# Coefficient tiles in DRAM laid out by row pairs instead of by single steps

## The chip, the cores and the metric

The kernel runs on one core of one Trainium2 chip. The metric is the device time of one execution in microseconds. Before the change it is 2900.72 us, the median of three runs (2892.87, 2900.72 and 2903.77). The profiled execution took 2902.61 us.

## The reference

Four layers run over x of shape (4, 64, 256, 256) in float32: batch, channels and images of 256 x 256. Layers 0, 2 and 3 are long convolutions with separable filters; layer 1 works on Haar coefficients. Cut to what matters:

```python
# layers 0, 2, 3: hx, hy are (256 x 64) filters from a small sine network
k = einsum('ijk,imk->ijmk', hx, hy)[0]            # separable per channel
y = irfft2(rfft2(x, 512, 512) * rfft2(k, 512, 512))[..., :256, :256]
out = y + x * bias[:, None, None]                  # causal 2-D convolution
# layer 1
f1 = haar2d(x)                                     # all levels, rows and columns
for i in range(2):
    f4 = einsum('bchw,oc->bohw', f1 * v[i], conv_w[i])      # mixes the 64 channels
    acc += sign(f4) * relu(abs(f4) - tau[i])
y = haar2d(acc, inverse=True) + x
```

The convolutions and the Haar transforms work on one image of one channel. The mixing of layer 1 needs all 64 channels of a coefficient row at once.

## The kernel before

The batch is cut into GROUPS = 2 groups of NB = 2 images. Each group has ROUNDS = 32 rounds of CI = 2 channels, so that a round holds four images: 128 partitions of 2048 floats (8 KB). The first 64 partitions belong to the round's first channel and the others to its second (`half(e)`).

Three phases follow one another, and overlap:

- **Phase A** (64 rounds): for each round, load x (L133), convolve rows and columns as Toeplitz products on TensorE (L307), add the bias term (L470), run the Haar transform along the free dimension on GpSimd (L355, L357) and along the partitions on TensorE (L319), copy the result to a tile f (L483), and store f to the DRAM tile coef of its group (L488, in `store`).
- **Phase B** (64 steps per group): a step has all 64 channels of two coefficient rows: 128 partitions (row, channel) of NB x 512 floats, 4 KB. `load` brings ft from coef (L546) and v and tau (L552). Two units per step mix the channels on TensorE (L592), multiply by v (L603), and apply the threshold (L609 to L619). GpSimd adds the two branches and the old coefficients (L629, L632), and the sum gt is stored to the DRAM tile mixed (L635).
- **Phase C** (64 rounds): load g from mixed (L699), run the inverse Haar transform (L375, L392, L394, L319), and then the two convolutions of layers 2 and 3 (L307), and store the output (L766).

So coef is written in rounds (two channels, all rows) and read in steps (two rows, all channels); mixed is written in steps and read in rounds. Each of the four DRAM tiles (coef and mixed of two groups) holds 64 x 512 KB, 32 MB.

Every DMA is issued from SP's queue, in the order in which the kernel's Python code runs; there is no scheduler behind it. Phase A of group 1 runs beside phase B of group 0, and phase B of group 1 beside phase C of group 0; `beside` interleaves the pieces of two lists by count. In a round the SP queue gets six loads of Toeplitz filters (tx and ty, 64 KB each, L146), one load of x (1 MB), and the round's coefficient stores; beside phase B, also about two steps' ft, v, tau and mixed. SP issues in order: a DMA whose data or buffer is not ready holds all that follow. Each DMA also uses one of eight semaphores in turn, so that it is not issued before the DMA eight places ahead of it has landed. [...]

The layout of the DRAM tile coef (and mixed) before is (step, row of the pair, channel, image, two row blocks, column), L101. `rows_of` gives the 64 rows of one channel in the steps of one parity, each 4 KB long; `all_rows` makes four pairs of a DRAM pattern and an SBUF part for a round: two channels, two parities. `step_of` gives a step, which is one contiguous piece of 512 KB.

Of the kernel before, what the change touches and what calls it, by code (L numbers as in the profile page):

```python
# [41 lines left out]
F32 = mybir.dt.float32  # L42
# [5 lines left out]
P = 128  # L48
B, C, N = 4, 64, 256

ROW = 64
# [14 lines left out]
NB = B // GROUPS  # L66
CI = 4 // NB
# [3 lines left out]
STEPS = C  # L71
# [3 lines left out]
W = 2 * N  # L75
# [14 lines left out]
def conv_haar_kernel(  # L90
# [6 lines left out]
    dram = ctx.enter_context(tc.tile_pool(name="dram", bufs=1, space=DRAM))  # L97


    def coefficients(name):  # L100
        return dram.tile([STEPS, 2, C, NB, 2, N], F32, tag=name, name=name)  # L101

    coef = [coefficients(f"coef{g}") for g in range(GROUPS)]
    mixed = [coefficients(f"mixed{g}") for g in range(GROUPS)]
    filt = [dram.tile([P, REPEATS, PERIOD], F32, tag=f"filt{l}", name=f"filt{l}") for l in range(NL)]

# [3 lines left out]
    def pool(name, bufs, stack=ctx, **kw):  # L110
        return stack.enter_context(tc.tile_pool(name=name, bufs=bufs, reuse_waits="tile", **kw))
# [188 lines left out]
    def half(r):  # L300
        return slice(r * ROW, (r + 1) * ROW)
# [110 lines left out]
        for _ in range(count):  # L412
            next(ops, None)

    def rows_of(dram_tile, c, bp):

        n = NB * W
        at = dram_tile.offset + (bp * 2 * C + c) * n
        return bass.AP(dram_tile.tensor, at, [[4 * C * n, ROW // 2], [C * n, 2], [1, n]])

    def all_rows(grp_tile, c0, images):

        parts = images.rearrange("p (s n) k -> p s (n k)", s=2)
        return [(rows_of(grp_tile, c0 + e, bp), parts[half(e), bp]) for e in range(CI) for bp in range(2)]

    def phase_a():

# [57 lines left out]
        def store(t):  # L485
            grp, c0 = t // ROUNDS, t % ROUNDS * CI
            for to, f in all_rows(coef[grp], c0, st[t]["f"]):
                nc.sync.dma_start(to, f)  # L488
            st[t].clear()
# [39 lines left out]
    def phase_b(grp):  # L529
# [6 lines left out]

        def step_of(ap, s):
            n = NB * W
            return bass.AP(ap.tensor, ap.offset + 2 * s * C * n, [[n, P], [1, n]])

        def load(s):
            if s >= STEPS:
                return
            d = st[s]
            d["f"] = bp.tile([P, NB, W], F32, tag="ft", name=f"ft_{grp}_{s}", bufs=4)
            nc.sync.dma_start(d["f"].rearrange("p b w -> p (b w)"), step_of(coef[grp], s))  # L546
            for name, src in (("v", v), ("tau", taus)):
                t = d[name] = bp.tile([P, 2, W], F32, tag=name, name=f"{name}_{grp}_{s}", bufs=3)

                at = src.offset + s * 4 * W * COPIES  # L550
                flat = bass.AP(src.tensor, at, [[2 * W, 2 * COPIES], [0, C // COPIES], [1, 2 * W]])
                nc.sync.dma_start(t.rearrange("p e w -> p (e w)"), flat)  # L552
# [81 lines left out]
        def store(s):  # L634
            nc.sync.dma_start(step_of(mixed[grp], s), st[s]["g"].rearrange("p b w -> p (b w)"))  # L635
            st[s].clear()
# [49 lines left out]
    def phase_c():  # L686
# [6 lines left out]
        def load(t):  # L693
            if t >= total:
                return
            grp, c0 = t // ROUNDS, t % ROUNDS * CI
            st[t]["g"] = big("in", f"g_{t}", 3)
            for rows, g in all_rows(mixed[grp], c0, st[t]["g"]):
                nc.sync.dma_start(g, rows)  # L699
# [133 lines left out]
    bp = pool("b", 2, during)  # L833
# [9 lines left out]
    bp = pool("b2", 2, during)  # L843
# [116 lines left out]
```

## Time and profile before

| | |
|---|---|
| median of three runs | 2900.72 us |
| profiled execution, device time | 2902.61 us |
| its span, first to last instruction | 2900.8 us |
| granted TensorE clock, mean | 0.943 |
| DMA packets | 239673, 636.27 MB, mean 219 GB/s |
| DMA queue q1 (all of SP's DMAs) | 239160 packets, 628.62 MB, 76.3% of 16 engines' span |
| HBM read, written | 413.12 MB, 215.35 MB |

The chain of work that ended last is given by the page as PE 45%, ACT 11%, DMA 10%, "issue" 8%, DVE 7%, POOL 4%, SP's queue 2%. Its largest lines are the four Toeplitz products of phase C with 8 to 9% each.

How to read it: PE is TensorE, PEld its weight loads, DVE VectorE, ACT ScalarE, POOL GpSimd, SP SyncE. A busy share over the span mixes stages with different limits; the phases A alone (0 to 470 us), A with B (to about 1210), B with C (about 1330 to 2200) and C alone have to be read one by one. A row of the DMA list names the tile written and the tile read, the number of DMAs, the KB of each, and the median time from issue to landing.

### The profile page before, as it was taken

How to read it: one execution, taken by the hardware profiler on the slowest of the kernel's cores; microseconds unless marked ns; L12 is line 12 of the kernel's file. 1: busy time of each engine (PE TensorE's matmuls, PEld its weight loads, DVE VectorE, ACT ScalarE, POOL GpSimd, SP SyncE). 2: the span in 40 equal slices, each digit the busy share in tenths (PEclk: the TensorE clock that was granted, in tenths of full speed). 3: DMA queues.
4: the chain of work that ended last, by engine and by line, in shares of the span. 5: the costliest groups of instructions: out<-in, count | busy, mean ns of one | idle time of the engine just before them, and what ended most of it. 6: DMA issues, size and time to landing. Idle time of an engine off the chain costs nothing.

```text
span 2900.8 us, 119451 instructions
## 1 busy us (share of the span) xinstructions
PE 2439.5 (84%) x53276; PEld 1966.7 (68%) x53276; DVE 1561.7 (54%) x1765; ACT 1523.6 (53%) x2361; POOL 1930.3 (67%) x2294
## 2 busy tenths in 40 slices
PE   6999886777776777868978888888888999999999
PEld 5777775444444544546757767666677889898888
DVE  2453333777777777537656766666673333333333
ACT  1222222666776666436767776666674333433332
POOL 2787674977887877738767766766675556555551
PEclk9999998988998888979999999999999999999999
DMA  5878888899999999777989888888975555655552
GB/s 153 238 212 228 235 237 228 244 284 289 296 291 284 276 300 281 217 182 224 252 238 251 252 231 248 239 243 242 253 211 159 142 151 137 155 143 146 146 141 92
DMA packets 239673, 636.27 MB, mean 219 GB/s; under 512 B 39078, under 2 KB 121671, under 8 KB 223032
## 3 DMA queue, kind: packets, MB, share of 16 engines
q1 hardware_dynamic: 239160, 628.62, 76.3%
q8 instruction: 420, 6.88, 1.0%
q14 instruction: 93, 0.76, 0.1%
HBM read 413.12 MB, written 215.35 MB: 217 GB/s over the span
## 4 chain that ended last, share of the span: by engine, by line
PE 45%; ACT 11%; DMA 10%; issue 8%; DVE 7%; POOL 4%; SPq 2%; ACTq 0%; DVEq 0%; POOLq 0%
PE c1r L307 9%; PE c1c L307 9%; PE c2c L307 9%; PE c2r L307 8%; PE f L592 4%; PE c0ps L319 3%; DVE f L603 3%; ACT m L609 3%; ACT f L612 3%; DMA v<-in_v 3%; ACT other L625 2%; DMA ft<-coef 2%; POOL fw L355 1%; POOL f L357 1%; ACT ch L740 1%
## 5 line engine op out<-in xcount | busy, mean ns | idle before, releaser
L392 POOL TENSOR_TENSOR i<-i,g 128x16 f32<-128x16 f32 x744 | 393.1, 549 | 407.5 <-ACT g L375 397.7
L616 DVE TENSOR_TENSOR f<-f,tau 128x1024 f32<-128x1024 f32 x256 | 314.8, 1230 | 384.0 <-ACT f L612 384.0
L592 PE MATMUL f<-ft,mix 64*64 64x512 f32 x2048 | 341.1, 662 | 189.4 <-DVE m L619 102.0
L609 ACT ACTIVATE m<-f 128x1024 f32<-128x1024 f32 x256 | 263.3, 1029 | 415.8 <-DVE f L603 400.3
L307 PEld LDWEIGHTS a1ps<-tx,x 64*64 64x64 f32 x8192 | 332.7, 144 | 146.9 <-ACT f L483 65.6
L629 POOL TENSOR_TENSOR gt<-m,ft 128x1024 f32<-128x1024 f32 x128 | 302.5, 2363 | 192.9 <-DVE m L619 167.0
L307 PE MATMUL a1ps<-tx,x 64*64 64x256 f32 (+3 forms) x8192 | 363.5, 320 | 56.1 <-ACT f L483 26.0
L307 PE MATMUL c2r<-tx,cy 64*64 64x128 f32 (+3 forms) x8192 | 332.1, 305 | 50.2 <-issue 36.8
L307 PE MATMUL c1r<-tx,z 64*64 64x192 f32 (+3 forms) x8192 | 338.5, 308 | 39.2 <-issue 39.2
L307 PEld LDWEIGHTS c2r<-tx,cy 64*64 64x64 f32 x8192 | 308.9, 137 | 81.4 <-issue 48.7
L603 DVE TENSOR_TENSOR f<-f,v 128x1024 f32<-128x1024 f32 x256 | 313.6, 1225 | 91.8 <-PE f L592 64.8
L307 PEld LDWEIGHTS c1r<-tx,z 64*64 64x64 f32 x8192 | 316.3, 139 | 68.8 <-issue 51.1
L307 PEld LDWEIGHTS c1c<-ty,ch 64*64 64x64 f32 x8192 | 307.7, 135 | 64.8 <-ACT z L728 47.3
L632 POOL TENSOR_TENSOR gt<-gt,other 128x1024 f32<-128x1024 f32 x128 | 302.4, 2363 | 70.6 <-ACT other L625 68.1
L307 PE MATMUL c2c<-ty,ch 64*64 64x128 f32 (+3 forms) x8192 | 323.2, 298 | 27.5 <-issue 25.2
L307 PE MATMUL c1c<-ty,ch 64*64 64x256 f32 (+3 forms) x8192 | 335.3, 303 | 10.9 <-ACT z L728 8.8
L307 PEld LDWEIGHTS a2ps<-ty,ay 64*64 64x64 f32 x8192 | 301.5, 137 | 62.1 <-issue 35.4
L307 PEld LDWEIGHTS c2c<-ty,ch 64*64 64x64 f32 x8192 | 304.0, 134 | 50.5 <-issue 31.2
L307 PE MATMUL a2ps<-ty,ay 64*64 64x192 f32 (+3 forms) x8192 | 328.3, 304 | 10.2 <-issue 6.4
L740 ACT COPY ch<-c1r 128x512 f32<-128x512 f32 x256 | 137.6, 590 | 371.4 <-PE c1r L307 371.0
L470 DVE SCALAR_TENSOR_TENSOR x<-x,bias_sb,a2ps 128x512 f32<-128x512 f32 x256 | 179.4, 741 | 268.4 <-PE a2ps L307 252.3
L619 DVE SCALAR_TENSOR_TENSOR m<-f,m 128x1024 f32<-128x1024 f32 x256 | 310.5, 1213 | 0.1
(66 smaller groups left out, 3257.9 us busy)
## 6 DMA issues: line engine op xcount, KB each, us to landing
coef<-f SPq DMA_DIRECT2D x256, 256.0 KB, 4.9
ft<-coef SPq DMA_DIRECT2D x128, 512.0 KB, 9.1
v<-in_v SPq DMA_DIRECT2D x128, 512.0 KB, 10.0
tau<-taus SPq DMA_DIRECT2D x128, 512.0 KB, 10.6
mixed<-gt SPq DMA_DIRECT2D x128, 512.0 KB, 7.8
g<-mixed SPq DMA_DIRECT2D x256, 256.0 KB, 6.9
x<-in_x SPq DMA_DIRECT2D x63, 1024.0 KB, 9.7
out<-o SPq DMA_DIRECT2D x63, 1024.0 KB, 4.8
```

What stands on the lines that cost most here:

```text
L307: nc.tensor.matmul(ps[r][half(c), j % 2, k * ROW :], data[half(r), c, k, bass.ts(j, ROW)], t(r, c)[:, : N - k * ROW], start=k == 0, stop=k ...
L319: nc.tensor.matmul(ps[r][half(c)].rearrange("p h k -> p (h k)"), matrix[half(r)], pairs(r, c).rearrange("p h k -> p (h k)"), start=True, s ...
L392: engine.tensor_tensor(to, s, d, op)
L470: nc.vector.scalar_tensor_tensor(to, old, bias_sb[:, c : c + 1], ps, ALU.mult, ALU.add)
L592: nc.tensor.matmul(un[u]["f4"][half(to), i, :], mixers[0][half(q), bass.ts(i, C)], f[half(q), u % 2], start=True, stop=True, tile_position ...
L603: nc.vector.tensor_tensor(f4, f4, st[u // 2]["v"], ALU.mult)
L609: nc.scalar.activation(un[u]["m"], un[u]["f4"], AF.Sign)
L616: nc.vector.tensor_tensor(f4, f4, st[u // 2]["tau"], ALU.subtract)
L619: nc.vector.scalar_tensor_tensor(un[u]["m"], un[u]["f4"], 0.0, un[u]["m"], ALU.max, ALU.mult)
L629: nc.gpsimd.tensor_tensor(st[s]["g"], st[s]["m"][:, :, 0], st[s]["f"], ALU.add)
L632: nc.gpsimd.tensor_tensor(st[s]["g"], st[s]["g"], st[s]["other"], ALU.add)
L740: later(lambda y=y, ps=ps: nc.scalar.copy(y, ps))
```

## The change

The DRAM tiles coef and mixed get another order of dimensions: (pair of steps, row, channel, step of the pair, image, two row blocks, column). The two steps of a pair are now beside one another for each row and channel, and make 8 KB together. A round stores or loads, for each of its two channels, 64 rows of 8 KB in one DMA: two DMAs of 512 KB in place of four of 256 KB. A step of phase B still is 128 rows of 4 KB, now 8 KB apart instead of contiguous. `rows_of` is gone; its pattern stands in `all_rows`.

```diff
     def coefficients(name):
-        return dram.tile([STEPS, 2, C, NB, 2, N], F32, tag=name, name=name)
+        return dram.tile([STEPS // 2, 2, C, 2, NB, 2, N], F32, tag=name, name=name)
...
-    def rows_of(dram_tile, c, bp):
-
-        n = NB * W
-        at = dram_tile.offset + (bp * 2 * C + c) * n
-        return bass.AP(dram_tile.tensor, at, [[4 * C * n, ROW // 2], [C * n, 2], [1, n]])
-
     def all_rows(grp_tile, c0, images):
 
-        parts = images.rearrange("p (s n) k -> p s (n k)", s=2)
-        return [(rows_of(grp_tile, c0 + e, bp), parts[half(e), bp]) for e in range(CI) for bp in range(2)]
+        n = 2 * NB * W
+        pairs = []
+        for e in range(CI):
+            at = grp_tile.offset + (c0 + e) * n
+            rows = bass.AP(grp_tile.tensor, at, [[2 * C * n, ROW // 2], [C * n, 2], [1, n]])
+            pairs.append((rows, images[half(e)].rearrange("p n k -> p (n k)")))
+        return pairs
...
         def step_of(ap, s):
             n = NB * W
-            return bass.AP(ap.tensor, ap.offset + 2 * s * C * n, [[n, P], [1, n]])
+            return bass.AP(ap.tensor, ap.offset + (s // 2 * P * 2 + s % 2) * n, [[2 * n, P], [1, n]])
```

The order of all other instructions on every engine stays as it was. The lines below the change move up by one: the round's store is L487 after, L488 before.

## The prediction

> **What bounds the kernel now.** I read the page's head and its list of DMA issues first, then busy time by stage, then the chain of waits by stage, and last the SP queue instruction by instruction. The head and the issue list:
>
> ```profile
> PE 2439.5 (84%) x53276; PEld 1966.7 (68%) x53276; DVE 1561.7 (54%) x1765; ACT 1523.6 (53%) x2361; POOL 1930.3 (67%) x2294
> ...
> coef<-f SPq DMA_DIRECT2D x256, 256.0 KB, 4.9
> ft<-coef SPq DMA_DIRECT2D x128, 512.0 KB, 9.1
> ...
> mixed<-gt SPq DMA_DIRECT2D x128, 512.0 KB, 7.8
> g<-mixed SPq DMA_DIRECT2D x256, 256.0 KB, 6.9
> ```
>
> The change touches these four rows and no engine's work. Next, stages of 200 us (columns: window, length, busy time of PE, PEld, DVE, ACT, POOL, granted clock, DMA share, GB/s):
>
> ```profile
> 200.00:400.00 200.00, 182.54 (x4296) 149.72 (x4299) 69.61 (x97) 53.12 (x96) 151.36 (x252) 0.99 0.85 235
> ...
> 600.00:800.00 200.00, 147.99 (x2430) 97.97 (x2426) 151.56 (x146) 141.78 (x173) 155.05 (x159) 0.89 0.96 289
> ...
> 1400.00:1600.00 200.00, 167.17 (x3528) 136.38 (x3523) 132.77 (x139) 138.10 (x201) 141.17 (x131) 0.93 0.90 250
> ...
> 2400.00:2600.00 200.00, 196.41 (x5252) 178.87 (x5248) 69.58 (x100) 77.48 (x170) 113.15 (x160) 1.00 0.57 148
> ```
>
> Phase A alone (to 470 us) is at 91% PE. With phase B beside it (470 to 1210) the DMA engines are 96% busy and no compute engine is over 78%: transfers decide there. From 1330 to 2200 (B beside C) PE leads again, and from 2200 phase C alone is PE and nothing else. The late part of phase A in the SP queue (start, length, line, operation, count):
>
> ```profile
> 437.39 0.70 SPq L133 DMA_DIRECT2D x<-in_x  x1
> 438.14 4.20 SPq L146 DMA_DIRECT2D tx<-filt  x4
> 442.45 1.16 SPq L146 DMA_DIRECT2D ty<-filt  x2
> 444.04 4.18 SPq L488 DMA_DIRECT2D coef<-f  x4
> 448.31 1.44 SPq L133 DMA_DIRECT2D x<-in_x  x1
> ```
>
> SP issues without a pause here, and the next x waits behind four coefficient stores. Each DMA takes one of eight semaphores in turn, so an issue also waits until the DMA eight places before it has landed: the trace has the second coef store of this group released at 446.3 by the landing of the x issued at 437.4. What one issue costs (min/median/max ns):
>
> ```profile
> L488 SPq DMA_DIRECT2D coef<-f x256: 512/617/2587, 71.3 to 1264.5; - x128
> L546 SPq DMA_DIRECT2D ft<-coef x128: 319/386/1944, 471.4 to 2143.9; - x128
> ```
>
> ```profile
> L699 SPq DMA_DIRECT2D g<-mixed x256: 507/607/2486, 1204.1 to 2814.9; - x128
> L635 SPq DMA_DIRECT2D mixed<-gt x128: 319/428/1539, 532.6 to 2188.8; - x128
> ```
>
> A pattern of rows and runs (ft, mixed) costs some 390 to 430 ns, coef stores and g loads some 610.
>
> [...] Its packet records show g loads (64 partitions) alone on the queues at 2411 to 2414 us with 16 packets in flight, 188 to 238 GB/s; coef stores at 418.5 to 420.5 us move 180 to 221; 1 KB rows of tx and ty back to back 199 to 246; 128-partition loads at 699 to 702 us some 400. So a 4 KB packet that takes 159 ns elsewhere takes about 305 in coef and g. [...] the change doubles the bytes of a DMA and keeps 64 partitions. [...] Coef rows lie 512 KB apart, on average before and exactly after; no run shows another pitch here.
>
> **The change part by part.** (1) Round stores and loads: 4 DMAs of 64 rows x 4 KB become 2 of 64 rows x 8 KB, 128 DMAs less for coef and 128 less for g. The four-dimensional walk over row pairs also collapses to 64 equally spaced rows. SP's spacing from one issue's start to the next, where a DMA follows directly, has a median of 0.71 us for coef, 0.66 for g, 0.38 for the two-dimensional mixed store. I take 0.68 before and 0.38 after: 4 x 0.68 - 2 x 0.38 = 1.9 us of SP freed per round, 128 times, some 245 us of SP time in all. Bounds for the new issue: 0.33 (mixed's shortest 319 ns and a few ns of gap) and 0.66 (as before), so 1.4 to 2.1 us per round.
>
> (2) DMA work: the bytes stay. [...] a round's coefficients keep 256 x 305 ns / 16 = 4.9 us of the 16 DMA engines; 128 packets of 8 KB at twice that are the same 4.9. At full rate 8 KB takes 309 against 2 x 159 = 318 ns, 3% less. 256 DMAs less also save 4096 semaphore packets of 12 ns, 3 us over all engines' time. I cost this at zero; bounds below in the rivals.
>
> (3) Phase B's ft loads and mixed stores: the same 128 rows of 4 KB, now every 8 KB in DRAM instead of back to back. Before has both shapes: the first x load reads 4 KB pieces every 8 KB and its packets have a median of 159 ns, three quarters of them below 170; the tau copies write 2 KB pieces 32 KB apart at 84 ns, the full rate. Issue stays two-dimensional. Zero, with bounds 0 and +60 ns per packet.
>
> (4) Windows: 17 DMAs instead of 19 per round in phases A and B together, 15 instead of 17 in C, so eight slots hold more bytes. Reading the list, tx and ty still wait on the same ft, v, tau and mixed; it is the DMAs behind coef that get free sooner. The second coef store still waits for x, and a slot is held for 512 KB instead of 256.
>
> What lies on the path, by stage. Phase A alone: over 371 to 470 us the chain of waits gives SPq L488 4.1% of 99 us, 4.1 us; two cheap issues leave 1.2, so -3, and -2 for the earlier rounds, where PE hides nearly all of it: -5. A and B together: the 60 us of SP freed in 32 rounds is covered by the busy transfers; it can only fill the 4 to 5% of DMA idle time, 33 us in 740, mostly where tx and ty hold six of eight slots, which stays. I take a fifth: -7. Handover (1210 to 1330): SPq is 17.7 us of the chain; eight g loads become four (8 x 0.66 - 4 x 0.38 = 3.8 us) and the last coef stores likewise; -5. B beside C: two chain pieces on g landings, -1. C alone: hidden by PE at 98%, and stays so, as no transfer is late: 0. Sum -18 us.
>
> The profiled execution took 2902.6 us (span 2900.8 and 1.8 around it); it lies 1.9 above the median of the three runs. 2902.6 - 18 = 2884.6; from the median 2882.7. I say 2884.
>
> **The rivals.** *Nothing measurable* (chance 0.28): the saved SP time is covered everywhere, -5 or so, 2896. For it: [...] the last 700 us are PE. Against: the chain runs through SP issues in late A and the handover.
>
> *[...]* (0.10): [...] 8 KB rows run at 309 ns. Then coef needs 2.5 us of the engines per round instead of 4.9; 32 rounds under B give 77 us, of which I count half since the compute chain takes over, on top of the 18: about 2845. [...]
>
> *Slower* (0.18): the strided halves in phase B. If ft and mixed packets take 60 ns more [...], 64 steps x 256 packets x 60 / 16 = 61 us of DMA work fall in the stage at 96%, three quarters on the path, +46 - 18: about 2930. It ends above before from 24 ns per packet, and 0.5% above from 43. In the second B group PE hides it. Only the load side is shown under light traffic, so I don't exclude it.
>
> **How the numbers follow.** Forecast 0.44 (2884, own range 2870 to 2894), the three rivals 0.28, 0.10, 0.18. A measurement tells 0.5%, 14.5 us, from no change; the limits are 2886 and 2915. The forecast lies just beyond the limit: 0.40 of it counts as faster, with 0.10 of the packet rival, and 0.02 of the quiet one makes 0.52. The slower rival reaches its limit in most of its cost range: 0.16. The rest, 0.32, is same. The range leaves out a tenth at either end: 2848 to 2922.
>
> **What would show it.** Right: coef and g rows with half the DMAs, 512 KB each, issue medians near 380 ns; ft and mixed landing times as before; SPq L487 in late A's chain down to a third; the 600 to 1200 us stage still at 95% DMA and some 1% shorter; C alone unchanged. In the packet records, 8 KB packets near 610 ns in coef and g. Wrong: 8 KB packets near 309 [...], ft and mixed above 159 where 128-partition traffic runs alone (the stride costs), or issues that still cost 600 ns.

## The result, and the profile after

The changed kernel takes 2978.89 us, the median of four runs (2971.62 to 2990.31); the kernel before, run beside it, takes 2899.92. The ratio is 1.0279, with a 95% interval of 1.0234 to 1.0323: slower by 2.8%. The profiled execution took 2972.22 us, against 2902.61 before.

The page's head, the rows of the DMA list, the instruction queue and the group that multiplies ft, all of the kernel after:

```profile
PE 2470.2 (83%) x53276; PEld 1981.9 (67%) x53276; DVE 1565.2 (53%) x1765; ACT 1522.5 (51%) x2361; POOL 1930.6 (65%) x2294
...
q8 instruction: 420, 6.88, 1.0%
...
L591 PE MATMUL f<-ft,mix 64*64 64x512 f32 x2048 | 345.7, 675 | 194.7 <-DMA ft<-coef 88.3
...
coef<-f SPq DMA_DIRECT2D x128, 512.0 KB, 6.5
ft<-coef SPq DMA_DIRECT2D x128, 512.0 KB, 11.6
...
mixed<-gt SPq DMA_DIRECT2D x128, 512.0 KB, 9.5
g<-mixed SPq DMA_DIRECT2D x128, 512.0 KB, 10.2
```

The change did what it says: coef and g have half the DMAs at twice the size, and the compute engines execute the same instructions (53276 matmuls and weight loads each). But ft lands 11.6 us after its issue instead of 9.1, and mixed 9.5 instead of 7.8. Of the idle time ahead of the mixing matmuls, 88.3 us now end with ft's landing, more than with any other releaser. Before, DVE led, and ft accounted for 38.8 us. PE is busy 30.7 us longer for the same instructions. The same group before:

```profile
L592 PE MATMUL f<-ft,mix 64*64 64x512 f32 x2048 | 341.1, 662 | 189.4 <-DVE m L619 102.0
```

Next the same stages as before the change, and the stretch from 600 to 1200 us as a whole, first after and then before (columns: window, length, busy time of PE, PEld, DVE, ACT and POOL, granted clock, DMA share, GB/s):

```profile
200.00:400.00 200.00, 181.56 (x4237) 147.26 (x4232) 70.14 (x98) 52.16 (x94) 149.24 (x247) 0.99 0.85 236
600.00:1200.00 600.00, 432.41 (x6754) 278.45 (x6745) 427.71 (x406) 399.82 (x490) 446.41 (x452) 0.86 0.96 276
1400.00:1600.00 200.00, 164.79 (x3519) 136.70 (x3518) 133.47 (x138) 136.25 (x199) 137.53 (x127) 0.95 0.88 240
2400.00:2600.00 200.00, 186.41 (x4921) 167.35 (x4923) 66.17 (x95) 71.95 (x157) 108.00 (x149) 0.99 0.53 136
```

```profile
600.00:1200.00 600.00, 439.26 (x7274) 292.60 (x7270) 440.33 (x421) 419.10 (x516) 472.40 (x476) 0.90 0.95 287
```

Two of these stages show a loss at once. From 600 to 1200 us the DMA engines are as busy as before (0.96 against 0.95) but move 276 GB/s instead of 287, and every engine gets through fewer instructions: the transfers themselves became slower. The granted clock fell as well, from 0.90 to 0.86. In these four stages it is lower where PE is busy less (0.99 at 91 and 93% busy, 0.95 at 82%, 0.86 at 72%), so it is read as a consequence: a slow PE alone would leave the DMA engines idle, and they are busy (0.96). No run separates the two. From 2400 to 2600 us PE executes 4921 matmuls instead of the 5252 of before, and the DMA engines are half idle.

The start of the same issue in both traces gives the loss by stage (us from the span's start):

```
                                      before     after    later by
first ft of group 0                    471.4     472.2       0.8
first ft of group 1                   1268.1    1298.7      30.6
out of phase C, round 0               1332.2    1359.6      27.4
out of phase C, round 32              2283.6    2329.5      45.9
out of phase C, round 56              2770.9    2840.2      69.3
end of the span                       2900.8    2970.4      69.6
```

Phase A alone loses nothing that shows, phase B beside A 29.8 us, phase C beside B 18.5, and the 24 rounds of phase C alone between the last two milestones 23.4.

Here is TensorE in that last stage, from the timeline of the kernel after (start, length, line, operation, form, count; in brackets the idle time before it and what ended it):

```profile
2542.01 4.58 PE L307 MATMUL c2r<-tx,cy 64*64 64x256 f32 x125
2548.35 1.95 PE L319 MATMUL c0ps<-ci,inverse_sb 64*64 64x512 f32 x16 [1.76 <-issue]
...
2563.42 4.03 PE L307 MATMUL c2r<-tx,cy 64*64 64x256 f32 x106
2569.52 0.65 PE L307 MATMUL c2r<-tx,cy 64*64 64x192 f32 x14 [2.07 <-issue]
```

PE stops for 1.76 and 2.07 us, in the second case in the middle of the matmuls of one product, and no semaphore releases it ("issue"). What ends such a pause shows in the packet records. The queue q8, "instruction", moves 420 packets of 16 KB. Its 6.88 MB over the 106552 matmuls and weight loads are 64.6 bytes for each, and in each 200 us of the trace of before one packet comes for 248 to 262 of them, so most of it is read as TensorE's own instruction stream. The packets near the two pauses ended at 2546.98 and 2568.16, that is 1.37 and 1.36 us before PE went on. In the trace of before, TensorE (matmuls and weight loads taken together) has 71 pauses over 0.5 us without a releaser. Of these, 67 end 1.1 to 1.75 us after the end of such a packet (median 1.46), 117 of 122 us in all; by chance it would be about one in ten, as 420 stretches of 0.65 us make up 9% of the span. After the change it is 91 of 95 pauses, 164 of 167 us. So PE is read as waiting for its instructions in these pauses (the expectations below call them fetch stalls), and the page counts that queue, 1.0%, on the same 16 DMA engines as the data's 76.2%. Over the whole span such pauses of more than 0.3 us make 121 us before the change already, and 167 after it.

### The profile page after: what moved, and what is told of

The parts are those of the page before. It is cut to its first block, busy times and chain, and to the rows that moved or that the text cites. A ratio compares the mean times of both kernels' runs of the same rounds, so it can differ in the third digit from the quotient of the medians.

```text
span 2970.4 us, 118894 instructions
## 1 busy us (share of the span) xinstructions
PE 2470.2 (83%) x53276; PEld 1981.9 (67%) x53276; DVE 1565.2 (53%) x1765; ACT 1522.5 (51%) x2361; POOL 1930.6 (65%) x2294
## 3 DMA queue, kind: packets, MB, share of 16 engines
q1 hardware_dynamic: 218680, 628.61, 76.2%
q8 instruction: 420, 6.88, 1.0%
## 4 chain that ended last, share of the span: by engine, by line
PE 45%; DMA 15%; ACT 9%; issue 7%; DVE 6%; POOL 4%; SPq 1%; ACTq 0%; DVEq 0%; POOLq 0%
PE c2c L307 9%; PE c1r L307 9%; PE c1c L307 9%; PE c2r L307 8%; DMA v<-in_v 4%; PE f L591 4%; PE c0ps L319 3%; DMA ft<-coef 3%; DVE f L602 3%; ACT m L608 2%; DMA mixed<-gt 2%; ACT f L611 2%; ACT other L624 2%; DMA x<-in_x 2%; DMA coef<-f 2%
## 5 line engine op out<-in xcount | busy, mean ns | idle before, releaser
L591 PE MATMUL f<-ft,mix 64*64 64x512 f32 x2048 | 345.7, 675 | 194.7 <-DMA ft<-coef 88.3
L307 PE MATMUL a1ps<-tx,x 64*64 64x192 f32 (+3 forms) x8192 | 372.1, 322 | 50.8 <-ACT f L482 22.8
L307 PE MATMUL c1r<-tx,z 64*64 64x256 f32 (+3 forms) x8192 | 340.6, 310 | 51.8 <-issue 51.7
L307 PE MATMUL c2r<-tx,cy 64*64 64x256 f32 (+3 forms) x8192 | 330.1, 304 | 37.4 <-issue 32.5
L307 PE MATMUL c2c<-ty,ch 64*64 64x128 f32 (+3 forms) x8192 | 329.4, 302 | 36.6 <-issue 34.9
L307 PEld LDWEIGHTS c2c<-ty,ch 64*64 64x64 f32 x8192 | 310.7, 136 | 59.7 <-issue 41.7
L307 PE MATMUL a2ps<-ty,ay 64*64 64x256 f32 (+3 forms) x8192 | 333.8, 306 | 16.1 <-issue 12.0
## 6 DMA issues: line engine op xcount, KB each, us to landing
ft<-coef SPq DMA_DIRECT2D x128, 512.0 KB, 11.6
```

The costliest lines, as they stand in the source:

```text
L307: nc.tensor.matmul(ps[r][half(c), j % 2, k * ROW :], data[half(r), c, k, bass.ts(j, ROW)], t(r, c)[:, : N - k * ROW], start=k == 0, stop=k ...
L591: nc.tensor.matmul(un[u]["f4"][half(to), i, :], mixers[0][half(q), bass.ts(i, C)], f[half(q), u % 2], start=True, stop=True, tile_position ...
```

## The experiments

Two properties of the change can be set independently. One is the pitch of phase B's rows: 4 KB pieces lie every 8 KB (the change) or back to back. The other is the number of DMAs in which a round's 1 MB of coefficients moves: two of 512 KB (the change) or four of 256 KB. All ratios are to the kernel before, run beside each on the same chip, whose median lay between 2894.8 and 2897.3.

### One part at a time

*pairs, four DMAs* keeps the new layout and has a round's four DMAs back:

```diff
+        parts = images.rearrange("p (s n) k -> p s (n k)", s=2)
...
-            at = grp_tile.offset + (c0 + e) * n
-            rows = bass.AP(grp_tile.tensor, at, [[2 * C * n, ROW // 2], [C * n, 2], [1, n]])
-            pairs.append((rows, images[half(e)].rearrange("p n k -> p (n k)")))
+            for bp in range(2):
+                at = grp_tile.offset + (2 * (c0 + e) + bp) * n
+                rows = bass.AP(grp_tile.tensor, at, [[4 * C * n, ROW // 2], [2 * C * n, 2], [1, n]])
+                pairs.append((rows, parts[half(e), bp]))
```

> The layout of after (step pairs together, phase B's rows 4 KB at an 8 KB pitch), but a round moves four DMAs of 64 rows x 4 KB, as before. Ratio to before. Stride theory (B's pitched rows cost): 1.02 to 1.03, as after. Packet theory (the 8 KB packets cost): 0.995 to 1.005. Queue theory (two DMAs of 512 KB in eight slots cost): 0.995 to 1.005.

*planes, two DMAs* has a third layout, in which each parity of steps has a plane of its own. A step is contiguous again, and a round still uses two DMAs of 512 KB, in pieces of 4 KB:

```diff
-        return dram.tile([STEPS // 2, 2, C, 2, NB, 2, N], F32, tag=name, name=name)
+        return dram.tile([2, STEPS // 2, 2, C, NB, 2, N], F32, tag=name, name=name)
...
-            rows = bass.AP(grp_tile.tensor, at, [[2 * C * n, ROW // 2], [C * n, 2], [1, n]])
+            rows = bass.AP(grp_tile.tensor, at, [[C * n, ROW], [ROW * C * n, 2], [1, n]])
...
-            return bass.AP(ap.tensor, ap.offset + (s // 2 * P * 2 + s % 2) * n, [[2 * n, P], [1, n]])
+            return bass.AP(ap.tensor, ap.offset + (s % 2 * STEPS // 2 + s // 2) * P * n, [[n, P], [1, n]])
```

> A third layout: one plane for each step parity. Phase B's steps are contiguous, as before; a round moves two DMAs of 512 KB made of 4 KB pieces. Ratio to before. Queue theory: 1.02 to 1.03. Packet theory and stride theory: 0.995 to 1.005.

*planes, four DMAs* is that layout with one plane per DMA, so that each issue is a plain two-dimensional one:

```diff
-            at = grp_tile.offset + (c0 + e) * n
-            rows = bass.AP(grp_tile.tensor, at, [[C * n, ROW], [ROW * C * n, 2], [1, n]])
-            pairs.append((rows, images[half(e)].rearrange("p n k -> p (n k)")))
+            for bp in range(2):
+                at = grp_tile.offset + (bp * ROW * C + c0 + e) * n
+                rows = bass.AP(grp_tile.tensor, at, [[C * n, ROW], [1, n]])
+                pairs.append((rows, parts[half(e), bp]))
```

> The layout by planes with four DMAs of 64 rows x 4 KB per round at one even pitch of 256 KB, B contiguous. It changes only the row pattern of the round DMAs (two-dimensional, so a cheaper issue, 0.33 to 0.4 us instead of 0.6). All three theories: 0.99 to 1.005. Below 0.995 would say that the issue time of SP counts.

*pairs, padded* keeps the change's two DMAs and its dimensions, but puts 512 bytes behind each 4 KB, so that the rows of a step lie 9 KB apart; the 8 KB of a row are then no longer one piece:

```diff
+PAD = 128
...
-        return dram.tile([STEPS // 2, 2, C, 2, NB, 2, N], F32, tag=name, name=name)
+        return dram.tile([STEPS // 2, 2, C, 2, NB * W + PAD], F32, tag=name, name=name)
```

> After, with 512 bytes of padding behind each step's 4 KB, so that a round's two DMAs of 512 KB consist of 4 KB packets; B's rows at a pitch of 9 KB. Ratio to before. Packet theory: 0.995 to 1.005. Queue theory and stride theory: 1.02 to 1.03.

Measured: pairs with four DMAs 2932.45 us, ratio 1.0123 (1.0096 to 1.0151); planes with two 2933.16, 1.0127 (1.0096 to 1.0159); planes with four 2892.14, 0.9986 (0.9971 to 1.0001); pairs padded 2937.27, 1.0142 (1.0113 to 1.0170). Each part of the change costs some 1.3%, and without both nothing remains; none of the three theories on record explains the change by itself. The cheaper issue that was expected of the planes with four did not come: its median is 617 ns for coef and 606 for g, against 617 and 607 before. From the planes with four, 0.0137 for the pitch and 0.0141 for the size give 1.0264, close to the 1.0279 of the change.

The stretch from 600 to 1200 us, of pairs with four DMAs, and then of planes with two:

```profile
600.00:1200.00 600.00, 430.24 (x6792) 277.24 (x6794) 423.45 (x401) 400.16 (x492) 447.53 (x454) 0.86 0.96 275
```

```profile
600.00:1200.00 600.00, 440.01 (x7316) 292.50 (x7312) 442.38 (x422) 419.27 (x517) 473.98 (x478) 0.90 0.96 288
```

The slow transfers go with the 8 KB pitch (275 GB/s), and not with the DMAs' size (288). The page's group of the mixing matmuls says the same: with pairs and four DMAs ft's landing leads their idle time, with planes and two DMAs it does not.

```profile
L593 PE MATMUL f<-ft,mix 64*64 64x512 f32 x2048 | 346.0, 675 | 198.7 <-DMA ft<-coef 90.5
```

```profile
L591 PE MATMUL f<-ft,mix 64*64 64x512 f32 x2048 | 333.3, 650 | 172.7 <-DVE m L618 93.4
```

The rounds 32 to 56 of phase C alone, the same work in each, in this order: before, after, planes with two DMAs.

```profile
2284.00:2771.00 487.00, 475.15 (x12673) 430.75 (x12668) 168.12 (x240) 186.17 (x408) 273.09 (x384) 1.00 0.56 146
```

```profile
2330.00:2840.00 510.00, 482.57 (x12661) 431.06 (x12657) 168.17 (x240) 185.93 (x408) 272.88 (x384) 0.99 0.54 139
```

```profile
2290.00:2799.00 509.00, 485.19 (x12692) 432.70 (x12688) 168.14 (x241) 186.03 (x408) 272.91 (x384) 0.99 0.55 139
```

Here it is the size: 509 us with contiguous steps and two DMAs, as after. DVE, ACT and POOL do the same work in the same time in all three, and the DMA share of 0.54 to 0.56 leaves room. PE alone is late. That stage has only g loads among the DMAs that the change made larger.

### Which transfers carry the pitch

*four DMAs, pitch in the loads only* has coef in pairs and mixed in planes, so that ft is read in 8 KB steps but mixed is written contiguously:

```diff
-            for to, f in all_rows(coef[grp], c0, st[t]["f"]):
+            for to, f in pair_rows(coef[grp], c0, st[t]["f"]):
...
-            nc.sync.dma_start(d["f"].rearrange("p b w -> p (b w)"), step_of(coef[grp], s))
+            nc.sync.dma_start(d["f"].rearrange("p b w -> p (b w)"), pair_of(coef[grp], s))
```

> Four DMAs per round; coef in pairs (phase B's ft loads at the 8 KB pitch), mixed in planes (its stores contiguous). If the pitched loads carry e1's loss: 1.010 to 1.015; if the pitched stores do: 0.997 to 1.003; if both by half: about 1.006.

Measured: 2922.19 us, 1.0104 (1.0074 to 1.0134). From 600 to 1200 us it moves 278 GB/s, and phase B beside A takes 819.5 us, against 794.0 with the planes and 828.4 with the pitch in both. The loads carry most of it. Three kernels that are alike in this stage (planes with four, and below load eight when alone and B in halves) lie between 789 and 794 us. What the stores add, 8.9 us between single profiles and 1.0123 against 1.0104 with overlapping intervals, is not established.

### Packet size or DMA size

A two-DMA round has larger packets too. *row pad* leaves everything as in the change, 8 KB pieces included, and puts 512 bytes behind each 8 KB row:

```diff
-        return dram.tile([STEPS // 2, 2, C, 2, NB, 2, N], F32, tag=name, name=name)
+        return dram.tile([STEPS // 2, 2, C, 2 * NB * W + PAD], F32, tag=name, name=name)
...
-            rows = bass.AP(grp_tile.tensor, at, [[2 * C * n, ROW // 2], [C * n, 2], [1, n]])
+            rows = bass.AP(grp_tile.tensor, at, [[C * m, ROW], [1, n]])
...
+            m = 2 * n + PAD
+            return bass.AP(ap.tensor, ap.offset + s // 2 * P * m + s % 2 * n, [[m, P], [1, n]])
```

> After with 512 bytes of padding behind each row of 8 KB: a round's two DMAs of 8 KB packets stay, phase B's rows lie 8.5 KB apart instead of 8. If the exact 8 KB pitch carries half of the loss: 1.012 to 1.017, and 600 to 1200 us at 284 GB/s or more. If any stride costs: 1.025 to 1.03 and 277 GB/s. If 8 KB packets cost something of their own, it is what lies above e4's 1.0142.

*row pad, quarters* moves the same 8 KB pieces in four DMAs of 32 rows:

```diff
+            for r in range(2):
+                at = grp_tile.offset + (c0 + e + r * h * C) * m
+                rows = bass.AP(grp_tile.tensor, at, [[C * m, h], [1, n]])
+                part = images[e * ROW + r * h : e * ROW + (r + 1) * h]
+                pairs.append((rows, part.rearrange("p n k -> p (n k)")))
```

> e9 with each round DMA cut by rows: four DMAs of 32 rows x 8 KB. The packets stay at 8 KB[...]. If the size of a DMA is what delays the instruction fetch: 0.997 to 1.004, and rounds 32 to 56 of phase C take 485 to 490 us. If the packet size is: 1.012 to 1.017 and 505 to 512 us.

Measured: row pad 2946.21 us, 1.0182 (1.0155 to 1.0210); in quarters 2893.99, 0.9991 (0.9972 to 1.0011). The row pad's stretch from 600 to 1200 us:

```profile
600.00:1200.00 600.00, 432.46 (x7191) 287.26 (x7186) 435.73 (x417) 413.08 (x511) 475.52 (x480) 0.90 0.96 288
```

With 8.5 KB between rows the rate is back at 288 GB/s: what costs is a pitch of exactly 8 KB, not the gaps. And the same 8 KB packets cost nothing in four DMAs, so the other loss does not belong to the packets. It goes with the number of DMAs in which a round's bytes move, and so with their size. Whether 8 KB packets add a little in large DMAs stays open: 1.0182 with them, 1.0142 with 4 KB (pairs, padded), with intervals that touch and another pad.

### The semaphore slots

*planes, two DMAs, with slots* adds to the planes with two a DMA of 64 bytes behind each of a round's stores and loads, so that the eight semaphores turn as fast as with four:

```diff
+    def slot():
+
+        used.append(0)
+        nc.sync.dma_start(slots[len(used) - 1], wcol_sb[:16, :1])
```

> e2 (planes, two DMAs of 512 KB per round) with a DMA of 64 bytes behind each of them, so that a round takes four of the eight slots again, with the same data in DMAs of 512 KB. Slot theory (two DMAs let more transfers into the queue): 0.997 to 1.003, as e3. Share theory [...]: 1.009 to 1.015, as e2, with 25 us or more of fetch stalls after 2220 us.

Measured: 3072.00 us, 1.0606 (1.0578 to 1.0634). Neither expectation fits, that of the slots or that of the size of one DMA (there the share theory). The 256 small DMAs cost 5% themselves: phase A alone ends 31 us later than with the planes with two, and phase B beside A takes 889 us instead of 797. But the rounds 32 to 56 come down to 492 us from 509, and PE's pauses in them from 21.9 to 14.6 us, although the DMAs of data are as large as before. So the size of one DMA is not the whole of what goes with the pauses. A small DMA turns the semaphores, and its issue (602 ns in the median) also keeps the next large one back; the experiment does not separate these two.

### The size alone, store by store and up to eight

*store two, load four* (planes) has the coef stores of a round in two DMAs and the g loads in four:

```diff
-            for to, f in all_rows(coef[grp], c0, st[t]["f"]):
+            for to, f in two_rows(coef[grp], c0, st[t]["f"]):
```

> Planes; coefficient stores as two DMAs per round, g loads as four. e2's loss lies in phase C by its trace, so both theories: 0.995 to 1.003. Over 1.008 would say that the stores cost.

*load eight* (planes, coef in four) loads g by single images, eight DMAs of 128 KB in pieces of 2 KB:

```diff
-            for rows, g in all_rows(mixed[grp], c0, st[t]["g"]):
+            for rows, g in image_rows(mixed[grp], c0, st[t]["g"]):
```

> Planes; coefficient stores as four DMAs, g loads as eight DMAs of 128 KB with 2 KB rows[...]. Share theory: fetch stalls after 2220 us fall from 13.8 to below 10 us, ratio 0.990 to 0.998 unless the four more issues per round cost SP too much. Slot theory: g takes all eight slots, filters come later, 0.995 to 1.01.

*load eight when alone* does so in group 1 only, whose phase C has no phase B beside it:

```diff
-            for rows, g in image_rows(mixed[grp], c0, st[t]["g"]):
+            for rows, g in (all_rows if grp == 0 else image_rows)(mixed[grp], c0, st[t]["g"]):
```

> Planes, four coefficient stores; g as four DMAs in group 0 (beside phase B) and eight of 128 KB in group 1 (phase C alone). Rounds 32 to 56 as in e7, 476 to 481 us; no SP load added beside B. Ratio 0.991 to 0.997.

*B in halves* goes on from there and cuts ft, v, tau and mixed of group 1's phase B, which runs beside a TensorE-bound phase C, into two DMAs of 256 KB each:

```diff
+        def in_parts(sb, flat):
+            if grp == 0:
+                return [(sb.rearrange("p b w -> p (b w)"), flat)]
+            dims = [list(d) for d in flat.ap[:-1]] + [[1, W]]
+            return [(sb[:, i], bass.AP(flat.tensor, flat.offset + i * W, dims)) for i in range(2)]
...
-            nc.sync.dma_start(d["f"].rearrange("p b w -> p (b w)"), step_of(coef[grp], s))
+            for to, rows in in_parts(d["f"], step_of(coef[grp], s)):
+                nc.sync.dma_start(to, rows)
```

> e11, and phase B of group 1 (beside C) moves ft, v, tau and mixed as two DMAs of 256 KB each. If large DMAs delay the instruction fetch there too, stalls between 1210 and 2220 us fall from some 95 us to 50 to 70 and the ratio to 0.98 to 0.993; if eight slots then hold too little, 1.0 or more.

Measured: store two, load four 2900.62 us, 1.0018 (1.0002 to 1.0034); load eight 2884.41, 0.9960 (0.9944 to 0.9975); load eight when alone 2874.61, 0.9928 (0.9900 to 0.9957); B in halves 2842.95, 0.9827 (0.9797 to 0.9857). The last is faster than both kernels of the case.

Against the 0.9986 of the planes with four, two large stores cost some 0.3%, and two large loads on top of them (1.0127) a further 1.1%. So it is mainly the g loads that matter, in the stage where PE has little slack.

The rounds 32 to 56 and the stretch from 1400 to 2100 us of B in halves; before, the latter had 12421 matmuls at 245 GB/s:

```profile
1400.00:2100.00 700.00, 619.55 (x12980) 495.74 (x12975) 481.41 (x496) 505.22 (x750) 505.23 (x474) 0.96 0.89 255
2234.00:2713.00 479.00, 473.47 (x12661) 431.67 (x12656) 168.11 (x240) 185.02 (x408) 273.41 (x384) 1.00 0.54 148
```

These are 4.5% more matmuls in the same time beside B (12980 against 12421), with more DMAs and the same bytes. About half of that can be scatter of single profiles: load eight when alone has 12674 there and the planes with four 12394, though they are alike in that stage. The whole times decide: 0.9827 against 0.9928, with intervals that lie apart. The pauses between 1210 and 2220 us came down further than expected, to 30.2 us. What larger DMAs lose, smaller ones than the kernel's own gain.

### All kernels side by side

From the traces (us): the length of phase B beside A, from the first ft of group 0 to that of group 1; the rounds 32 to 56 of phase C; and the pauses of TensorE over 0.3 us that have no releaser and end 1.1 to 1.75 us after an instruction packet, in those rounds and in the whole span.

```
                          B rows     DMAs of   B beside  C alone  pauses  pauses
                          every      a g load  A         32-56    there   in all
before                    4 KB       4         797       487      11.3    121
after                     8 KB       2         827       511      23.6    167
pairs, four DMAs          8 KB       4         828       488      11.9    100
planes, two DMAs          4 KB       2         797       509      21.9    153
planes, four DMAs         4 KB       4         794       487      11.3    122
pairs, padded             9 KB       2         801       512      23.8    166
two with slots            4 KB       2+small   889       492      14.6    139
store two, load four      4 KB       4         793       486       9.2    139
load eight                4 KB       8         806       478       4.1     74
pitch in loads only       8 / 4 KB   4         820       486      10.8    138
row pad                   8.5 KB     2         796       513      27.9    177
row pad, quarters         8.5 KB     4         793       491      13.4    136
load eight when alone     4 KB       4 / 8     789       477       3.7     95
B in halves               4 KB       4 / 8     791       480       5.5     50
```

The fourth column follows the pitch: 820 to 828 where ft's rows lie every 8 KB, 789 to 806 with every other pitch, if the kernel with extra DMAs is left aside. The fifth follows the number of DMAs: 509 to 513 with two, 486 to 491 with four, 477 to 480 with eight, and 492 for two with small ones between. The pauses there go the same way, 22 to 28, 9 to 13, and 4 to 6 us. The last column scatters more: the two kernels with four DMAs and the pitch in both or in the loads only have 100 and 138.

The pauses in the table explain 12.3 of the 23.3 us between before and after in these rounds. Two more after the change, 3.4 us, also end 1.1 to 1.75 us after an instruction packet, but the profile puts them down to ACT and DVE. Most of the rest is PE itself: 482.57 us busy against 475.15 for the same matmuls, at a granted clock of 0.99 against 1.00. The four kernels with two g DMAs and nothing between them have 481 to 485 us, those with four or eight 473 to 477. The clock's record shows a part of it: in these rounds after the change, the granted clock is 0.5 in three stretches of 3.4 us, which is some 5 us of work by estimate (3 x 3.4 / 2). Each of these stretches begins within 1.3 us of the end of a pause of 2.05 to 2.67 us, and the kernels with four or eight g loads have none there. That order speaks for the pauses as the cause, but not every long pause is followed by one: the row pad has a pause of 3.2 us without.

Why the pauses are longer with two DMAs than with four shows in part. In rounds 33 to 55, nine in ten of the first instruction packets after the issue of an out store start within 6.4 us before the change, within 8.5 after it, and within 4.9 with eight loads. The order of the three numbers is that of the sizes of a g load (256, 512 and 128 KB). Why they follow it was not shown.

A second reading fits at least as well: the pace at which SP puts the bytes into the queue. In every round g is issued right behind the out store of 1 MB, and fewer issues bring its 1 MB in sooner. The same place in a round from SP's timeline, after the change and before it:

```profile
2539.26 0.33 SPq L765 DMA_DIRECT2D out<-o  x1
2539.70 1.89 SPq L698 DMA_DIRECT2D g<-mixed  x2
```

```profile
2506.41 0.34 SPq L766 DMA_DIRECT2D out<-o  x1
2506.85 3.27 SPq L699 DMA_DIRECT2D g<-mixed  x4
```

From the start of the out store's issue to the end of the last g issue it is 2.3 to 2.6 us (medians of rounds 33 to 55) in the kernels with two DMAs, 3.2 in the one with small DMAs between, 3.4 in row pad, quarters, 3.7 in the others with four, and 7.1 to 7.2 with eight. The times of rounds 32 to 56 follow in this order: 509 to 513, 492, 491, 486 to 488, and 477 to 480 us. In two with slots, which has DMAs of 512 KB, nine in ten of these packets start within 6.4 us, as before the change. The pace covers that and the size of one DMA by itself does not, but no run changes the pace alone.

## Why the prediction was wrong

Steps (3) and (4) failed, and the gain of step (1) did not exist.

- **(1) SP's issues.** The price of one issue was mis-sized, and the time saved had no worth. An issue of coef takes 552 ns in the median and one of g 848, and the shortest 446 and 444, where 0.38 us was taken for both; the bounds were 0.33 and 0.66. From the groups by tile of the kernel after (min/median/max ns):

```profile
L487 SPq DMA_DIRECT2D coef<-f x128: 446/552/2817, 70.5 to 1291.2; - x128
```

```profile
L698 SPq DMA_DIRECT2D g<-mixed x128: 444/848/2686, 1230.2 to 2882.7; - x128
```

  The 0.38 us came from few cases. In the trace of before it holds for the 16 mixed stores that another DMA follows within 0.08 us; over the 97 that one follows within 0.2 us the spacing is 0.63. As half of the issues are gone, SP still spends 217 us on those of coef and g instead of 425. That frees 1.6 us per round, inside the bounds of 1.4 to 2.1. Late in phase A the store's share of the chain of waits fell too, from 4.1% to 1.2%. The time did not: the first ft starts 0.8 us later than before, and kernels alike in phase A scatter there from 468 to 478 us, so that a gain of 5 us could not have been seen. PE was 91% busy there, and what the chain showed for SP was not a cost that goes away with it. The planes with four DMAs say nothing on this, as their issues cost what they did before. Row pad, quarters says something: with before's number and size of DMAs, SP spends 364 us on these issues, 61 us less than before, and the ratio is 0.9991 (0.9972 to 1.0011). Beside phase A the planes with two DMAs, which have no pitch, take 797 us as before, where -7 was forecast. The handover, from the first ft of group 1 to the first out store, is 60.9 us instead of 64.1, but 60.6 with the planes with four too, whose issues are not cheaper. So the -5, -7 and -5 us should have been near nothing, as the first rival had it.
- **(2) DMA work.** Right. With 8.5 KB rows, packets of 8 KB move as many GB/s as 4 KB packets did (288 against 287), and at 2541.8 to 2543 us after the change, where g moves, a packet of 8 KB takes 632 ns in the median, near the 610 of the forecast; the rival with 8 KB rows at 309 ns is out. Why packets of coef and g take about twice the 159 ns of other 4 KB packets (315 at 2411 to 2414 us before the change) was not shown.
- **(3) The strided halves of phase B.** "Zero, with bounds 0 and +60 ns per packet" failed: the pitch of exactly 8 KB costs 1.0 to 1.5% by the kernels that differ in it (1.0123 against 0.9986 with four DMAs; 1.0279 against 1.0127, 1.0142 and 1.0182 with two), most of it beside phase A. An estimate of its price: with the pitch in the loads only, B beside A took 25.5 us longer than with the planes; times 16 engines over that group's 8192 ft packets this is 50 ns each. Against the lowest of the kernels alike in that stage (789 us) it is 59. That is inside the bounds, near their upper end. The rival *Slower* named this stride and this place, and its +46 us is of the right size (29.8). It still ended at 2930 because it set -18 us against it, which did not come, and had nothing for phase C. The evidence for zero was the first x load, read at the same 8 KB pitch on idle queues. The prediction itself says that this side is shown under light traffic alone, and took the value from it all the same.
- **(4) Windows, and C alone.** "Hidden by PE at 98%, and stays so, as no transfer is late: 0" is the step that failed outright, and no rival covered it. No late transfer of data shows for TensorE there, but 23.6 us of pauses that end behind an instruction packet do, against 11.3 before. The loss is 23.4 us in 24 rounds. How much of the 18.5 us beside B is due to the same is not shown. Rounds 0 to 32 take 959 to 976 us in the four kernels with two DMAs and nothing between them, and 942 to 961 in those whose g loads there are four. The pauses between 1210 and 2220 us grew from 98.7 to 120.4, but pairs with four DMAs has 65.8 there and takes as long as before (950 against 951). The trace of before already held the sign: 71 pauses of PE with "issue" behind them and a queue named "instruction" on the DMA engines. A share of 1.0% for that queue looked like nothing. It says how much the queue moves, not how long TensorE pauses beside it (121 us before the change).

So the forecast was wrong in its sign, and 2979 lies above the range's 2922: some 40 us come from the pitch and some 40 from fewer and larger DMAs (0.0137 and 0.0141 times 2900), and the saved issues give nothing back.

Of what was to show it: from 600 to 1200 us the DMA engines stayed at 95 to 96%, but phase B beside A was longer, and ft and mixed landed later. Longer ft and mixed transfers were named as the sign that the stride costs.

## What to carry to other kernels

A DMA that is hidden behind a TensorE-bound stage can still have a price, as the pauses of 22 to 28 us with two g loads show here, against 9 to 13 with four. Look for PE pauses that end on "issue", set them against the packets of the instruction queue, and try more and smaller DMAs there before fewer and larger ones. In phase C alone, where the DMA engines are 0.53 to 0.57 busy, going from 512 to 256 and to 128 KB for g gained at every step (509 to 513, 486 to 491, 477 to 480 us for 24 rounds). Time that an issuing queue saves can be worth nothing (61 us less of SP and a ratio of 0.9991 in row pad, quarters), and by the order of the kernels here it may bring the bytes in too fast for something that is. When a layout is changed for one side, price the other side under the load of its own stage. Where rows come to lie exactly 8 KB apart, try a pad: 512 bytes and 1 KB between rows both removed the cost here (796 and 801 us beside phase A against 827), and no other pitch that is a power of two was tried in phase B's strided rows.

## What was unexpected in the hardware

- TensorE goes on 1.46 us (median before the change; 1.41 after it) after the end of a 16 KB instruction packet in 67 of the 71 pauses over 0.5 us without a releaser (91 of 95 after it). Such pauses over 0.3 us took 121 us of 2901 before the change, and 50 of 2842 in the fastest kernel.
- Reading 4 KB rows every 8 KB under full load leaves 275 to 278 GB/s for the stage as a whole, against 284 to 289 at pitches of 4, 8.5 and 9 KB. The mean 4 KB packet from 600 to 1200 us takes 228 ns with the pitch and four DMAs, and 217 with the planes and four, all queues together. Why a pad of 512 bytes behind each row suffices was not examined.
- 256 DMAs of 64 bytes cost 1.0606 against 1.0127, some 140 us, or 0.54 us each; SP's issue of one takes 602 ns in the median.
- An issue of 64 rows of 8 KB was not cheaper than one of 128 rows of 4 KB: 552 and 848 ns against 504 for ft and 354 for mixed, although all are two-dimensional once equal steps are merged.
